# A four-layer transformer on one core: the fourth layer's bias in two one-pass parts, and maxima of two layers taken off over all 128 partitions

## The chip, the cores and the metric

The kernel runs on one core of a Trainium2 chip. The metric is the device time of one execution in microseconds (us), the median over several runs. A core has one engine for matrix products (TensorE, PE in the profile, with its weight loads as PEld), three for elementwise work (VectorE or DVE, ScalarE or ACT, GpSimd or POOL) and SyncE (SP), which here only issues DMA transfers.

## What is computed

Input `x` is (8, 512, 128) in float32: 8 batches of 512 tokens. Four layers follow, each `x = x + attention(norm(x)) + experts(norm(x))`. Layers 0, 2 and 3 have a softmax attention with 16 heads of 8 channels, layer 1 a linear attention. Layers 0 and 2 are causal; in layer 2 the masked scores are not left out of the softmax but set to a large negative number. Layer 3 is not causal and adds a relative bias:

```python
energy = jnp.einsum('bhqd,bhkd->bhqk', q, k)
rel = jnp.clip(pos[:, None] - pos[None, :] + (N - 1), 0, bias_table.shape[0] - 1)
energy = energy + bias_table[rel].transpose(2, 0, 1)[None]
att = jax.nn.softmax(energy / (scaling * temp), axis=-1)
out = jnp.einsum('bhqk,bhkd->bhqd', att, v)
```

The table has 249 rows, and the bias equals its last row unless the key lies more than 263 tokens ahead of the query. The kernel takes this constant off, so that a bias is left only in the last two of the four blocks of 128 keys, for the first 128 and the first 256 queries.

## The kernel before

**Units.** `attention` makes one layer's attention, and `run` (from line 501) orders it. A unit is one batch and one group of four heads, 32 units in a layer. A unit goes through half-steps x: six in a causal layer, eight in layer 3. A half-step handles one block of 128 keys or queries, or two short ones, for two of the four heads, so its tile in PSUM is a pair: two banks of 128 x 512 (`ps_pair`, three buffers, shared by everything that uses pairs).

**Two passes over the scores.** Five units ahead of the output (`AHEAD = 5`), `first` (line 273) computes the scores `s` with queries on the partitions, and `first_rest` (line 289) adds the causal mask and takes row maxima on VectorE into `max`. In layer 3 it also adds the bias table `far[0]` there, on VectorE, in the last half-steps. `maxima` and `turn_maxima` split the 16 heads' maxima of a batch into a high and a low part and transpose them to `mT`: on partition 32h + 2g is the high part of head h in group g, on the next the low part.

`second` (line 341) computes the scores again, transposed, with keys on the partitions, into `t`. The maxima are taken off by a product that accumulates into the same bank: a matrix `pick` of zeros and two rows of ones selects the high and low row of a head and spreads it over all 128 keys. `second_rest` (line 367) adds, in layer 3, the transposed bias by a product with the identity (line 376), in layer 0 a mask (line 382), and then ScalarE takes the exponential to `p` (line 386). In layer 2 the mask is a select on GpSimd after the exponential. `weigh` (line 397) multiplies `p` with the values, `finish` and `divide` evict, transpose and normalise.

**Precision and passes.** Queries and keys are stored as high and low parts in a rounded float type (F32R), four parts of 8 channels, 32 rows for each head. So `first`, `second` and the `pick` product contract over 32 of the array's 128 rows, in one pass, and the two heads of a half-step use different rows and can run at the same time; `first` takes the other two heads' rows. `far`, `ident`, `p` and the values are plain float32. The trace shows each float32 product as two instructions, each of them two passes over its columns.

**Order.** In the loop over units, a half-step issues `first` of the unit five ahead, `second` of the present one, then `first_rest` and `second_rest`, other tasks that are due (`now`), and `weigh` after some half-steps. The order on TensorE is the order of the calls. Other engines' order is left to a scheduler.

**Layer 3's table.** `load_far` loads each of two tables of 128 x 16 x 256 (2 MB) from SyncE, `scale_far` takes off the last row and scales, head by head on VectorE, in place. `far[0]` is used by `first_rest`, `far[1]` by `second_rest`. `choose` picks two experts for a batch in layer 3 and gathers their weights `ws`; `inner3` and `outer3` use them.

Of the kernel before, what the change touches and what calls it, by code (L numbers as in the profile page):

```python
# [22 lines left out]
P = 128  # L23
# [18 lines left out]
def network(ctx: ExitStack, tc: tile.TileContext, io: dict):  # L42
# [11 lines left out]
    def ps_pair(name):  # L54
        return ps.tile([P, 2, T], F32, tag="pair", name=name, bufs=3)
# [53 lines left out]
    nmx = const.tile([P, NI, P], F32, name="nmx")  # L109
    nc.gpsimd.memset(nmx, 0.0)  # L110

    pick = const.tile([P, NG, P], F32R, name="pick")
    pick32 = wk.tile([P, NG, P], F32, tag="oT", name="pick32")
    nc.gpsimd.memset(pick32, 0.0)
    for j in range(HG):
        for r in range(2):
            nc.gpsimd.affine_select(
                pick32, pick32, pattern=[[-2, NG], [0, P]], compare_op=ALU.not_equal, fill=1.0,
                base=-32 * j - r, channel_multiplier=1,
            )  # L120
# [49 lines left out]
    anchor = {}  # L170


    def attention(L, w, causal, scale, bias=None, soft=None, vpad=None, add_masks=False):

# [98 lines left out]
        def first(b, g, x):  # L273

            pr = 1 - x % 2
            q, k = st[b]["q", g], st[b]["k", g]
            s = st["s"] = ps_pair(f"s{L}_{b}_{g}_{x}")
            for j in range(2):
                r = 32 * (2 * pr + j)
                for i, c, n in spans(x, True)[0]:  # L280
                    nc.tensor.matmul(  # L281
                        s[:, j, c : c + n],
                        lhsT=q[r : r + 32, blk(i)],
                        rhs=k[r : r + 32, :n],
                        start=(c == 0),
                        stop=not causal,
                    )

        def first_rest(b, g, x):
            pr = 1 - x % 2  # L290
            m, s = st[b]["m"], st.pop("s")
            for i, c, n in spans(x, True)[0]:
                for j in range(2):
                    if causal:
                        nc.tensor.matmul(  # L295
                            s[:, j, c + n - P : c + n], lhsT=ident_bf, rhs=mask_qk, start=False,
                            stop=(i == spans(x, True)[0][-1][0]),
                        )
            for i, c, n in spans(x, True)[0]:
                e = 256 - 128 * i if bias is not None and i < 2 else 0  # L300
                anchor["vector"] = nc.vector.tensor_reduce(  # L301
                    m[:, i, g, 2 * pr : 2 * pr + 2], s[:, :, c : c + n - e], AX.X, ALU.max, negate=True
                ).ins
                for j in range(2 if e else 0):
                    h = 2 * pr + j
                    to = m[:, i, g, h : h + 1]
                    sum_ = small.tile([P, 256], BF16, tag="sum", name=f"sum{L}_{b}_{g}_{x}_{j}", bufs=1)
                    nc.vector.tensor_tensor_reduce(
                        sum_[:, :e], s[:, j, T - e : T], bias[0][:, g * HG + h, :e], -1.0, to, ALU.add, ALU.min, to
                    )  # L310
# [30 lines left out]
        def second(b, g, x):  # L341

            pr = x % 2
            q, key, mT = st[b]["q", g], st[b]["k", g], st[b]["mT"]
            s = st["t"] = ps_pair(f"t{L}_{b}_{g}_{x}")
            for k in range(2):
                r = 32 * (2 * pr + k)
                for j, c, n in spans(x, False)[0]:
                    nc.tensor.matmul(  # L349
                        s[:, k, c : c + n],  # L350
                        lhsT=key[r : r + 32, blk(j)],
                        rhs=q[r : r + 32, T - n : T],
                        start=(c == 0),
                        stop=False,
                    )
            for k in range(2):
                r = 32 * (2 * pr + k)
                for j, c, n in spans(x, False)[0]:
                    nc.tensor.matmul(  # L359
                        s[:, k, c : c + n],  # L360
                        lhsT=pick[r : r + 32, g, :],
                        rhs=mT[r : r + 32, T - n : T],
                        start=False,
                        stop=(j == pieces[x][-1] and not add_masks and not (bias is not None and j >= 2)),
                    )

        def second_rest(b, g, x):
# [3 lines left out]
            if bias is not None and pieces[x][0] >= 2:  # L371
                (j,) = pieces[x]
                for k in range(2):
                    h = g * HG + 2 * pr + k
                    n = 128 * (j - 1)
                    nc.tensor.matmul(  # L376
                        s[:, k, :n], lhsT=ident, rhs=bias[1][:, h, 256 - n :], start=False, stop=True
                    )
            if add_masks:
                for j, c, n in blocks:  # L380
                    for k in range(2):
# [119 lines left out]
    def run(layers, tasks, soft, normed=None, begun=0):  # L501
# [22 lines left out]
        with tc.manual_schedule(engines={mybir.EngineType.PE}):  # L524
# [9 lines left out]
            for u in range(AHEAD):  # L534
                _, b, g = units[u]
                for x in range(A.nh):
                    A.first(b, g, x)
                    A.first_rest(b, g, x)
                    if u == 1 and x == 0:
                        A.values(0)  # L540
                    if u == 1 and x == 3:
# [8 lines left out]
            for u, (A, b, g) in enumerate(units):  # L550
# [5 lines left out]
                for x in range(A.nh):  # L556
# [2 lines left out]
                        upto = -(-(x + 1) * F.nh // A.nh)  # L559
                        firsts, done = range(done, upto), upto  # L560
                    for y in firsts[:-1]:
                        F.first(fb, fg, y)
                        F.first_rest(fb, fg, y)
                    if firsts:
                        F.first(fb, fg, firsts[-1])
                    A.second(b, g, x)
                    if firsts:
                        F.first_rest(fb, fg, firsts[-1])
# [630 lines left out]
    att_w[3] = load_attention(3)  # L1199

    sizes = [("base", D), ("d1", 256)]
    f2 = lay.tile([P, sum(n for _, n in sizes)], F32, tag="weights", name="f2")
    cut, at = {}, 0
    for k, n in sizes:
        cut[k] = f2[:, at : at + n]
# [92 lines left out]

    last = l3.tile([P, NH], F32, name="last")
    nc.sync.dma_start(last, bcast_rows(io["a3_last"], NH))  # L1300
    far = [l3.tile([P, NH, 256], F32, name=f"far{k}") for k in range(2)]

    def load_far(k):
        nc.sync.dma_start(far[k], io["a3_far"][k])
# [10 lines left out]
    layer3 = attention(3, att_w[3], False, 1.0, bias=far, vpad=layer2.vpad)  # L1315

    f3s = {}

    def choose(b):
# [38 lines left out]

    def more23(at):
        for k in range(2):  # L1360
            at(1, 3 * k, load_far, k)
            for h in range(NH):
                at(4, 2 * (NH * k + h), scale_far, k, h)
        for b in range(NB):
# [107 lines left out]
```

## Time and profile before

Three runs took 2850.75, 2855.13 and 2861.95 us, median 2855.13. The profiled execution took 2855.47 us with a span of 2853.8 us. By stretches of its span, from the trace:

| us | what runs | TensorE busy, us | VectorE busy, us | ScalarE busy, us | granted clock of TensorE |
|---|---|---|---|---|---|
| 0 to 91 | opening: first scores of layer 0, routing | 56 | 69 | 12 | 0.69 |
| 91 to 485 | layer 0, attention | 356 | 224 | 156 | 0.79 |
| 485 to 903 | layer 0, attention with its experts | 359 | 89 | 208 | 1.00 |
| 903 to 962 | layer 0, end of attention | 48 | 11 | 29 | 0.69 |
| 962 to 1600 | layer 1 | 565 | 399 | 167 | 0.93 |
| 1600 to 1675 | layer 1 to 2 | 58 | 53 | 9 | 0.71 |
| 1675 to 2264 | layer 2, and first scores of layer 3 | 515 | 363 | 311 | 0.87 |
| 2264 to 2773 | layer 3 | 468 | 373 | 288 | 0.98 |
| 2773 to 2854 | end of layer 3 | 73 | 7 | 48 | 0.98 |

The granted clock is a mean over a stretch; in the trace it is 1 or 0.5 at any moment, so a mean of 0.79 says that 42% of the stretch ran at half clock. A matmul's duration in the trace is its latency, and matmuls overlap; how long a group holds the engine is read from the distance between starts. Costly groups that the change touches, by line: L359 (maxima, `t<-mT,pick`) 1536 matmuls, 265.1 us busy; L376 (bias, `t<-far,ident`) 256 of 256 columns and 256 of 128, 72.4 and 47.4 us; L386 (exponential) 640, 596.5 us; L301 (row maxima) 768, 664.7 us.

### The profile page before, as it was taken

Reading aid. Unit: us, or ns where it says so; the run is one execution under the profiler, and the core shown is the slowest. Engines: PE = TensorE matmul, PEld = TensorE weight load, DVE = VectorE, ACT = ScalarE, POOL = GpSimd, SP = SyncE. Lnnn points to the kernel's source line nnn. Section 1 sums busy time; section 2 is a strip of 40 time slices with the busy share of each in tenths; the row PEclk is TensorE's granted clock in tenths of the full one; section 3 lists DMA queues with packets and bytes.
Section 4 is the critical chain, followed back from the end, with each engine's and each line's share of the span. In section 5 each row is a group of like instructions: output and inputs, shape, how many; then the busy total and the mean of one; then the engine's idle time right before and its main releaser. Section 6 shows DMA issues by size and latency. Waiting matters only on the chain.

```text
span 2853.8 us, 45040 instructions
## 1 busy us (share of the span) xinstructions
PE 2498.7 (88%) x17094; PEld 1581.6 (55%) x17094; DVE 1587.6 (56%) x4014; ACT 1227.0 (43%) x1791; POOL 557.5 (20%) x742
## 2 busy tenths in 40 slices
PE   5889998888887888879999788888988899999999
PEld 3555555777775466667887654444443344444444
DVE  7666444222212376755555675666656677777760
ACT  1333444454454423212222135555654455555555
POOL 3006740000002255250000223333322200000000
PEclk7587789999999788899999778999898899999999
DMA  8314432555553211122232422222111111221200
GB/s 283 115 60 136 127 96 85 161 169 164 163 167 104 68 46 50 27 78 64 89 92 72 153 80 64 66 65 65 62 61 61 51 38 62 67 65 62 67 23 8
DMA packets 168633, 252.38 MB, mean 88 GB/s; under 512 B 21472, under 2 KB 92384, under 8 KB 168032
## 3 DMA queue, kind: packets, MB, share of 16 engines
q1 hardware_dynamic: 155744, 221.39, 24.9%
q0 software_dynamic: 12672, 28.10, 3.5%
q8 instruction: 136, 2.23, 0.3%
q14 instruction: 81, 0.66, 0.1%
HBM read 155.57 MB, written 93.85 MB: 87 GB/s over the span
## 4 chain that ended last, share of the span: by engine, by line
PE 46%; DVE 12%; ACT 4%; issue 3%; POOL 2%; DMA 2%; SPq 0%; POOLq 0%; ACTq 0%; DVEq 0%
PE o L403 6%; DVE max L301 5%; PE o L1046 5%; PE s L281 4%; PE t L376 3%; PE s L1023 3%; PE t L349 3%; PE rc L1247 3%; PE t L359 3%; PE qk L994 2%; PE y L757 2%; PE p L221 1%; PE h L961 1%; PE s L295 1%; PE h L963 1%
## 5 line engine op out<-in xcount | busy, mean ns | idle before, releaser
L301 DVE TENSOR_REDUCE max<-s 128x2 f32<-128x1024 f32 (+3 forms) x768 | 664.7, 885 | 399.2 <-PE s L295 278.1
L386 ACT ACTIVATE p<-t 128x1024 f32<-128x1024 f32 (+1 forms) x640 | 596.5, 938 | 580.5 <-PE t L382 228.3
L349 PE MATMUL t<-q,k 32*128 32x512 f32 (+3 forms) x1536 | 325.5, 452 | 100.0 <-ACT p L386 51.3
L281 PE MATMUL s<-k,q 32*128 32x512 f32 (+3 forms) x1536 | 328.9, 457 | 31.7 <-DMA k<-apartk 13.8
L403 PE MATMUL o<-p,vpad 128*32 128x512 f32 (+3 forms) x3072 | 347.9, 540 | 5.5 <-DVE at L440 3.2
L281 PEld LDWEIGHTS s<-k,q 32*128 32x128 f32 x1536 | 147.1, 204 | 320.4 <-issue 166.8
L771 POOL DMA_INDIRECT yk<-ys_d,slots x160 | 162.5, 1016 | 700.7 <-DMA ys_d<-y 520.9
L359 PE MATMUL t<-mT,pick 32*128 32x512 f32 (+3 forms) x1536 | 265.1, 370 | 0.0
L349 PEld LDWEIGHTS t<-q,k 32*128 32x128 f32 x1536 | 148.0, 202 | 189.9 <-ACT p L386 81.2
L757 PE MATMUL y<-wt,h 128*128 128x128 f32 x1632 | 202.7, 278 | 23.1 <-DVE xsT L746 14.0
L757 PEld LDWEIGHTS y<-wt,h 128*128 128x128 f32 x1632 | 192.6, 192 | 33.7 <-issue 16.4
L723 POOL DMA_INDIRECT xs_d<-xr,slots x160 | 157.5, 985 | 189.6 <-DVE slots L715 136.5
L854 ACT ACTIVATE h<-h,wt 128x256 f32<-128x256 f32 x316 | 122.4, 477 | 135.7 <-issue 126.5
L1046 PEld LDWEIGHTS o<-v,a 128*128 128x128 f32 x1280 | 158.1, 197 | 27.4 <-issue 27.3
L852 PE MATMUL h<-xsT,wt 128*128 128x256 f32 x632 | 153.1, 385 | 21.7 <-DVE xsT L746 14.8
L390 POOL TENSOR_SCALAR_AFFINE_SELECT p<-p 128x256 f32<-128x256 f32 x256 | 101.8, 410 | 314.4 <-ACT p L386 313.1
L1046 PE MATMUL o<-v,a 128*128 128x65 f32 x1280 | 161.3, 279 | 0.0
L859 DVE TENSOR_TENSOR y<-y,wt 128x256 f32<-128x256 f32 x79 | 33.5, 424 | 218.9 <-PE y L757 215.6
L359 PEld LDWEIGHTS t<-mT,pick 32*128 32x128 f32 x1536 | 153.0, 210 | 1.2 <-issue 0.5
L1033 DVE TENSOR_TENSOR a<-s,decay 128x1024 f32<-128x1024 f32 (+3 forms) x128 | 99.9, 816 | 84.0 <-PE s L1023 83.6
L403 PEld LDWEIGHTS o<-p,vpad 128*32 128x32 f32 x3072 | 71.3, 113 | 134.5 <-issue 100.9
L295 PE MATMUL s<-mask_qk,ident_bf 128*128 128x128 bf16 x1024 | 140.9, 249 | 0.0
(258 smaller groups left out, 3591.5 us busy)
## 6 DMA issues: line engine op xcount, KB each, us to landing
wt<-in_f_w SPq DMA_DIRECT2D x79, 578.0 KB, 3.9
q<-apartq SPq DMA_DIRECT2D x96, 256.0 KB, 2.7
k<-apartk SPq DMA_DIRECT2D x96, 256.0 KB, 3.7
wt<-in_f_w SPq DMA_DIRECT2D x23, 768.0 KB, 5.0
xs<-xs_d SPq DMA_DIRECT2D x102, 128.0 KB, 3.2
ys_d<-y SPq DMA_DIRECT2D x102, 128.0 KB, 4.0
xs_d<-zero SPq DMA_DIRECT2D x50, 256.0 KB, 5.1
apartq<-highq SPq DMA_DIRECT2D x48, 256.0 KB, 2.9
```

The source lines that it names most:

```text
L281: nc.tensor.matmul(s[:, j, c : c + n], lhsT=q[r : r + 32, blk(i)], rhs=k[r : r + 32, :n], start=(c == 0), stop=not causal,)
L295: nc.tensor.matmul(s[:, j, c + n - P : c + n], lhsT=ident_bf, rhs=mask_qk, start=False, stop=(i == spans(x, True)[0][-1][0]),)
L301: anchor["vector"] = nc.vector.tensor_reduce(m[:, i, g, 2 * pr : 2 * pr + 2], s[:, :, c : c + n - e], AX.X, ALU.max, negate=True).ins
L349: nc.tensor.matmul(s[:, k, c : c + n], lhsT=key[r : r + 32, blk(j)], rhs=q[r : r + 32, T - n : T], start=(c == 0), stop=False,)
L359: nc.tensor.matmul(s[:, k, c : c + n], lhsT=pick[r : r + 32, g, :], rhs=mT[r : r + 32, T - n : T], start=False, stop=(j == pieces[x][-1] a ...
L386: nc.scalar.activation(p[:, :, :width], s[:, :, :width], AF.Exp, scale=scale)
L403: nc.tensor.matmul(st[b, g][blk(h, 32), T - n : T], lhsT=vpad[b % 2][:, j, g * HG + h, :], rhs=st[b, g, j, h // 2][:, h % 2, :], start=(j ...
L723: ins = nc.gpsimd.indirect_dma_start(out=xs_d, out_offset=bass.IndirectOffsetOnAxis(ap=slots[:, b * NI + i, k : k + 1], axis=0), in_=state ...
L757: nc.tensor.matmul(py[:, blk(k)], lhsT=h[:, f, blk(k)], rhs=out(wt)[:, f, :], start=(f == 0), stop=(f == 3))
L771: nc.gpsimd.indirect_dma_start(out=yk[:, k, :], out_offset=None, in_=ys_d, in_offset=bass.IndirectOffsetOnAxis(ap=slots[:, b * NI + i, k : ...
L852: nc.tensor.matmul(s[:, f, :], lhsT=wt[:, blk(f)], rhs=xsT, start=True, stop=True)
L1046: nc.tensor.matmul(o[:, k, i * 65 : i * 65 + 65], lhsT=lin[b, c, "a", j][:, k, blk(i - j)], rhs=v1[b % 2][:, j, 2 * c + k, :], start=(j == ...
```

## The change

- `pick` becomes a matrix of 128 partitions x 4 heads x 4 groups. A column of it is repeated 128 times by a broadcast read. In layers 0 and 2 (`whole=True`) the product that takes the maxima off contracts over all 128 partitions, with ones in the two rows of its head and zeros elsewhere; in layer 3 (`whole=False`) it stays on 32.
- The transposed bias of layer 3 is held as a high and a low part in F32R (`far_high`, and `far_low` with `far_rest`), and each is added by a one-pass product with an F32R identity. The second table comes in head by head, into a buffer of tag `oT`, which the evicted outputs use too, and is scaled and split on VectorE.
- In the opening of a run of layers, `first` is called for two half-steps before their `first_rest`.
- `f2` moves to another pool; the weights `ws` have two buffers in place of four, and `choose` runs at half-step 1 of unit u - 1 in place of half-step 3 of unit u - 2, counted from the batch's first unit.

```diff
-    pick = const.tile([P, NG, P], F32R, name="pick")
-    pick32 = wk.tile([P, NG, P], F32, tag="oT", name="pick32")
+    pick = const.tile([P, HG, NG], F32R, name="pick")
+    pick32 = const.tile([P, HG, NG], F32, name="pick32")
...
+            m = P if whole else 32
             for k in range(2):
-                r = 32 * (2 * pr + k)
+                r = 0 if whole else 32 * (2 * pr + k)
                 for j, c, n in spans(x, False)[0]:
                     nc.tensor.matmul(
                         s[:, k, c : c + n],
-                        lhsT=pick[r : r + 32, g, :],
-                        rhs=mT[r : r + 32, T - n : T],
+                        lhsT=pick[r : r + m, 2 * pr + k, g : g + 1].to_broadcast([m, P]),
+                        rhs=mT[r : r + m, T - n : T],
                         start=False,
...
                     n = 128 * (j - 1)
-                    nc.tensor.matmul(
-                        s[:, k, :n], lhsT=ident, rhs=bias[1][:, h, 256 - n :], start=False, stop=True
-                    )
+                    for part in range(2):
+                        nc.tensor.matmul(
+                            s[:, k, :n], lhsT=bias[2], rhs=bias[1](h)[part][:, 256 - n :], start=False, stop=part == 1
+                        )
...
                 for x in range(A.nh):
-                    A.first(b, g, x)
-                    A.first_rest(b, g, x)
+                    if x % 2 == 0:
+                        pairs = [A.first(b, g, x), A.first(b, g, x + 1)]
+                    A.first_rest(b, g, x, pairs[x % 2])
...
-    far = [l3.tile([P, NH, 256], F32, name=f"far{k}") for k in range(2)]
+    far = l3.tile([P, NH, 256], F32, name="far")
+    far_high = l3.tile([P, NH, 256], F32R, name="far_high")
+    rest = lay.tile([P, 10 * 256], F32R, tag="weights", name="far_rest")
+    low = (rest[:, : 9 * 256].rearrange("p (h c) -> p h c", h=9), l3.tile([P, 7, 256], F32R, name="far_low"))
+    ident_r = rest[:, 9 * 256 : 9 * 256 + P]
+    nc.gpsimd.tensor_copy(ident_r, ident)
...
     def scale_far(k, h):
-        t = far[k][:, h, :]
+        if k == 0:
+            nc.vector.tensor_scalar(far[:, h, :], far[:, h, :], last[:, h : h + 1], rsc, ALU.subtract, ALU.mult)
+            return
+        t = wk.tile([P, 256], F32, tag="oT", name=f"far_{h}")
+        nc.sync.dma_start(t, io["a3_far"][1][:, h, :])
         nc.vector.tensor_scalar(t, t, last[:, h : h + 1], rsc, ALU.subtract, ALU.mult)
+        nc.vector.tensor_copy(far_high[:, h, :], t)
+        nc.vector.tensor_tensor(low[h // 9][:, h % 9, :], t, far_high[:, h, :].bitcast(F32), ALU.subtract)
...
-        ws = f3s[b] = [weights_of(io["f3_ch"], place, l3, "ws", 4, f"{n}_{k}") for k, place in enumerate((first, second))]
+        ws = f3s[b] = [weights_of(io["f3_ch"], place, l3, "ws", 2, f"{n}_{k}") for k, place in enumerate((first, second))]
...
-            at(u - 2, 3, choose, b)
+            at(u - 1, 1, choose, b)
```

More of the change, by code (lines that the diff above doesn't have):

```diff
@@ L110, in network @@
     nc.gpsimd.memset(nmx, 0.0)
-    pick = const.tile([P, NG, P], F32R, name="pick")
-    pick32 = wk.tile([P, NG, P], F32, tag="oT", name="pick32")
+    pick = const.tile([P, HG, NG], F32R, name="pick")
+    pick32 = const.tile([P, HG, NG], F32, name="pick32")
     nc.gpsimd.memset(pick32, 0.0)
[L115 to L119, printed above, removed]
-            )
+    for r in range(2):
+        nc.gpsimd.affine_select(
+            pick32, pick32, pattern=[[-32, HG], [-2, NG]], compare_op=ALU.not_equal, fill=1.0, base=-r,
+            channel_multiplier=1,
+        )
     nc.gpsimd.tensor_copy(pick, pick32)
@@ L170, in network, with attention @@
     anchor = {}
-    def attention(L, w, causal, scale, bias=None, soft=None, vpad=None, add_masks=False):
+    def attention(L, w, causal, scale, bias=None, soft=None, vpad=None, add_masks=False, whole=True):
         st = {}
@@ L276, in first @@
             q, k = st[b]["q", g], st[b]["k", g]
-            s = st["s"] = ps_pair(f"s{L}_{b}_{g}_{x}")
+            s = ps_pair(f"s{L}_{b}_{g}_{x}")
             for j in range(2):
@@ L287, in first, with first_rest @@
                     )
-        def first_rest(b, g, x):
+            return s
+        def first_rest(b, g, x, s):
             pr = 1 - x % 2
-            m, s = st[b]["m"], st.pop("s")
+            m = st[b]["m"]
             for i, c, n in spans(x, True)[0]:
@@ L375, in second_rest @@
                     n = 128 * (j - 1)
-                    nc.tensor.matmul(
-                        s[:, k, :n], lhsT=ident, rhs=bias[1][:, h, 256 - n :], start=False, stop=True
-                    )
+                    for part in range(2):
+                        nc.tensor.matmul(
+                            s[:, k, :n], lhsT=bias[2], rhs=bias[1](h)[part][:, 256 - n :], start=False, stop=part == 1
+                        )
             if add_masks:
@@ L561, in run @@
                     for y in firsts[:-1]:
-                        F.first(fb, fg, y)
-                        F.first_rest(fb, fg, y)
+                        F.first_rest(fb, fg, y, F.first(fb, fg, y))
                     if firsts:
-                        F.first(fb, fg, firsts[-1])
+                        s = F.first(fb, fg, firsts[-1])
                     A.second(b, g, x)
                     if firsts:
-                        F.first_rest(fb, fg, firsts[-1])
+                        F.first_rest(fb, fg, firsts[-1], s)
                     A.second_rest(b, g, x)
@@ L1201, in network @@
     sizes = [("base", D), ("d1", 256)]
-    f2 = lay.tile([P, sum(n for _, n in sizes)], F32, tag="weights", name="f2")
+    f2 = l3.tile([P, sum(n for _, n in sizes)], F32, name="f2")
     cut, at = {}, 0
@@ L1300, in network, with far_parts @@
     nc.sync.dma_start(last, bcast_rows(io["a3_last"], NH))
-    far = [l3.tile([P, NH, 256], F32, name=f"far{k}") for k in range(2)]
+    far = l3.tile([P, NH, 256], F32, name="far")
[4 more added lines that the diff above has]
+    nc.gpsimd.tensor_copy(ident_r, ident)
+    def far_parts(h):
+        return far_high[:, h, :], low[h // 9][:, h % 9, :]
     def load_far(k):
-        nc.sync.dma_start(far[k], io["a3_far"][k])
+        nc.sync.dma_start(far, io["a3_far"][0])
     def scale_far(k, h):
-        t = far[k][:, h, :]
+        if k == 0:
[3 more added lines that the diff above has]
+        nc.sync.dma_start(t, io["a3_far"][1][:, h, :])
         nc.vector.tensor_scalar(t, t, last[:, h : h + 1], rsc, ALU.subtract, ALU.mult)
+        nc.vector.tensor_copy(far_high[:, h, :], t)
+        nc.vector.tensor_tensor(low[h // 9][:, h % 9, :], t, far_high[:, h, :].bitcast(F32), ALU.subtract)
     wr3 = const.tile([D, 8], F32, name="wr3")
@@ L1313, in network @@
     nc.sync.dma_start(br3, bcast_rows(io["f3_br"], 8))
-    layer3 = attention(3, att_w[3], False, 1.0, bias=far, vpad=layer2.vpad)
+    layer3 = attention(3, att_w[3], False, 1.0, bias=(far, far_parts, ident_r), vpad=layer2.vpad, whole=False)
     f3s = {}
@@ L1360, in more23 @@
         for k in range(2):
-            at(1, 3 * k, load_far, k)
+            if k == 0:
+                at(1, 0, load_far, k)
             for h in range(NH):
```

## The prediction

> **What bounds the kernel now.** I read the page first: TensorE's share, then the row of its granted clock.
>
> ```profile
> PE 2498.7 (88%) x17094; PEld 1581.6 (55%) x17094; DVE 1587.6 (56%) x4014; ACT 1227.0 (43%) x1791; POOL 557.5 (20%) x742
> ...
> PEclk7587789999999788899999778999898899999999
> ```
>
> TensorE is the bound at 88%, but its clock is not full in the slices of layer 0 (1 to 6), around 13 and in layer 2 (23 to 31). So I asked for the busy time by stretches: three attention units of layer 0 with the same work (g = 2 of three batches).
>
> ```profile
> 269.92:287.96 18.04, 16.40 (x119) 9.24 (x118) 8.52 (x19) 5.77 (x7) 13.65 (x15) 0.62 0.29 98
> 335.07:350.21 15.14, 13.78 (x118) 7.91 (x118) 8.31 (x19) 5.83 (x8) 11.48 (x13) 0.77 0.27 90
> 456.36:469.30 12.94, 11.29 (x118) 6.51 (x118) 8.13 (x19) 5.76 (x7) 0.00 (x0) 1.00 0.14 45
> ```
>
> The columns are length, busy time and count of PE, PEld, DVE, ACT and POOL, granted clock, DMA share and GB/s. Equal counts of matmuls take 12.94, 15.14 and 18.04 us at clocks 1.00, 0.77 and 0.62. The clock is either 1 or 0.5, so 0.62 means that 76% of 18.04 us (13.7 us) ran at half clock: each us at half clock loses (18.04 - 12.94)/13.7 = 0.37 us (the middle unit: 2.2/7.0 = 0.31). I take 0.36.
>
> What sets it? The clock changes on a grid of 3.41 us; three cells of it:
>
> ```profile
> 280.56:283.97 3.41, 3.41 (x25) 2.08 (x21) 1.38 (x4) 0.60 (x1) 2.80 (x3) 0.50 0.21 65
> 283.97:287.38 3.41, 3.41 (x28) 1.44 (x26) 1.06 (x3) 0.60 (x1) 2.49 (x4) 0.50 0.66 211
> 287.38:290.79 3.41, 2.66 (x26) 1.26 (x26) 1.97 (x2) 1.60 (x2) 2.50 (x4) 1.00 0.12 38
> ```
>
> In the first, TensorE has no gap at all and stays at half clock; only after the second is it full. Busy time is not what counts. The first cell holds, by form: 8 score products of 256 columns and 4 maxima products of 256, all on 32 of 128 rows, 5 masks and 4 two-pass transposes of 128 columns on all rows, and part of a group of 32-column products. I weighted each matmul by its share of the array, columns x passes x rows/128 x output columns/128, over the 8192 columns that a cell passes at full clock (a 512-column pass takes 0.215 us, from 1.72 us for the four two-pass products of L1340). The first cell gives 0.34, the second 0.405. Over all of the trace's cells this one number sorts the clock of the next cell: below 0.37 it is half, above it full, right in 99% of the cells at full and 97% of those at half clock. That is my reading of this trace, and most of the forecast rests on it.
>
> The other part lies in layer 3 (2264 to 2854 us), nearly always at full clock (0.98), with PE busy 468 of 509 us. First a half-step there, then one of layer 2:
>
> ```profile
> 2507.59 0.40 PE L359 MATMUL t<-mT,pick 32*128 32x512 f32 x2
> 2507.92 1.13 PE L376 MATMUL t<-far,ident 128*128 128x256 f32 x4
> 2508.98 0.50 PE L281 MATMUL s<-k,q 32*128 32x512 f32 x2
> ...
> 1900.76 0.50 PE L349 MATMUL t<-q,k 32*128 32x512 f32 x2
> ...
> 1901.10 0.39 PE L359 MATMUL t<-mT,pick 32*128 32x512 f32 x2
> ...
> 1901.42 0.11 PEld L295 LDWEIGHTS <-ident_bf 128*128 128x128 bf16 x2 [0.36 <-issue]
> ```
>
> Read the distance of the starts: the bias product of two heads takes 1.06 us at 256 columns (0.55 at 128); the maxima of two heads take 0.32 at 512, of which 0.215 is one pass (both heads at once, on different rows) and about 0.11 is the change of rows.
>
> [...]
>
> **The maxima in layers 0 and 2.** Per half-step the pair on 32 rows becomes two products on 128 rows, one after the other[...]. At 512 columns: 2 x 0.215 = 0.43 for 0.32, +0.11. At 384 + 128: 0.43 for 0.38 (1905.50 to 1905.88), +0.05. At 256: 0.215 for 0.21, nothing. Two half-steps of each in a unit: +0.32 us. PE waits for ACT 25 us of layer 0's attention and 22 of layer 2, so I put 60% on the path: 0.2 x 64 units = +13.
> The array share of these products becomes four times as large: in layer 0 they are 0.03 of a cell's 0.43, so 0.09 is added. The first cell above goes from 0.34 to 0.43: full clock. I laid the trace's matmuls out again with this share, the lengths above and the rule at 0.37. Layer 0's attention (91 to 485 us) goes from 165 us at half clock (2 x 0.21 x 394) to some 15, and its end (903 to 962) from 37 to 16; layer 2 (1675 to 2264, clock 0.87) from 153 to some 65. That is 259 us less, x 0.36 = -93. I keep 80% of it, since ACT and DVE, hidden behind a slow TensorE, come due: -74. Together with +13: -61.
>
> **The bias in layer 3.** A 256-column bias of two heads now is four products of one pass: 0.055 for the first weights, 4 x 0.11, 0.09 to drain: 0.58 for 1.06, -0.48. At 128: 0.35 for 0.55, -0.2. Two of each in a unit: -1.36 us, x 32 units = -43. DVE is late next: its half-steps here take 1.74 us (0.69 + 2 x 0.48 + 0.08), and PE's go from about 2.2 and 1.7 to 1.7 and 1.5. It waits for DVE already:
>
> ```profile
> PE t L349 <- DVE max L301: 17.9, 23, 1.4
> ...
> PE t L349 <- DVE max L308: 6.0, 14, 0.8
> ```
>
> The third buffer of pairs and the four light half-steps of a unit catch part; I count 75%: -32. The bias loses half of its array share, 0.07 of a cell's 0.59; laid out again, layer 3 has 10 to 20 us more at half clock: +5. No row shows a 128-row one-pass product in this type: bounds are one pass (taken, since 128 columns of it on 32 rows take as long as bf16's, 0.055) and two passes (no gain here).
>
> **The rest.** Splitting the table: 16 heads at 0.40 (the present scaling) plus a copy and a subtraction of that size, about +13 us of DVE in units 9 to 14, where it has room. Each scaling waits for a DMA of 128 KB issued beside it, landing in about 3 us, in a buffer shared with the evicted outputs: behind it on DVE queue the maxima, behind the buffer ACT's eviction, and on SP the q and k loads, a unit early. From 0 to 16 x 3 = 48; I take +6. The one 2 MB load becoming 16, the choice of experts three quarters of a unit later (two weight buffers; its landing of 2.8 us still has more than a unit), eight mask builds less on POOL (0.63 each, ahead of a gather at 19 us that waits for a DMA), the moved tile of 384 columns and the copy of the identity: nothing, -5 to +5. Pairs of first products in the opening: 15 times two products at once, DVE busy 29 of 35 us there: 0 to -5, I take 0.
>
> **Sum.** -61 - 32 + 5 + 6 = -82. The profiled execution took 2855.47 us, practically the median, 2855.13: 2773.
>
> **Rivals.** (A) As summed, 2773, its own range 2735 to 2815; 70%. (B) The clock hardly follows, because what is counted is not rows but something that goes with them in this trace: +13 - 43 x 0.75 + 6 = -13, 2842; with half of the clock's gain 2805; 12%. For it: the rule is a fit. Against: without the row share it sorts 92% of the cells at full and two thirds of those at half clock. (C) Layer 3 falls below the threshold: once at half clock, a cell with less than 0.37 keeps it there; at 200 us, +72 - 5 on top, 2840; 7%. Against: the median cell is at 0.59. (D) Slower: full-height one-pass products take two passes. The pair at 512 would be 0.86, 2.5 us more in a unit, x 64 x 0.6 = +95, with all of layer 3's gain gone, and the clock's -74: +27, 2882. It decides above 1.7 passes. 7%. (E) The table's DMAs hold up DVE at their upper bound: 2815; 4%.
>
> **How the numbers follow.** 0.5% (14 us) is what a measurement of this kernel tells from no change. Faster by more: A, C's better half, E, most of B: 0.86. Within: 0.07. Slower: D, 0.07. The range takes A with B's half gain and E: 2730 to 2825.
>
> **What would show it.** Clock of 91 to 485 above 0.93 (right) or still near 0.79 (B); starts of the two maxima products 0.215 apart (0.43: D); 512-column pair plus mask 0.11 later than before; the 256-column bias near 0.58; more waits of L349's line for DVE; layer 3's clock at 0.96 or more (below 0.9: C). I am wrong if the clock rises and units do not shorten.

## The result, and the profile after

The changed kernel took 2889.86 us in the median of nine runs (2867.96 to 2916.23), the kernel before 2854.87 us in as many (2840.2 to 2861.95): a ratio of 1.0119, 95% interval 1.0088 to 1.015. It is slower by 35 us, where 82 us less were forecast. A ratio here and below is an estimate over fast runs (three slow ones among the experiments are left out) and need not be the quotient of the two medians. The profiled execution took 2889.86 us too, with a span of 2888.2.

The page of the changed kernel, TensorE's share and the row of its clock in 40 slices:

```profile
PE 2534.7 (88%) x17094; PEld 1630.7 (56%) x17094; DVE 1607.2 (56%) x4046; ACT 1225.6 (42%) x1791; POOL 553.1 (19%) x737
...
PEclk7789999999999888899999789999999998999999
```

Slices 2 to 7 (layer 0) and those of layer 2 hold more nines than before: the clock rose where it was meant to. Yet TensorE is busy 36 us longer with the same number of instructions. The view by stretches (length, busy time and count of each engine, clock, DMA share, GB/s) for layer 0's attention, layer 2 and layer 3 of the changed kernel:

```profile
84.80:484.20 399.40, 360.60 (x3010) 223.35 (x3008) 223.47 (x553) 155.15 (x202) 133.00 (x136) 0.91 0.31 96
...
1684.70:2286.90 602.20, 540.01 (x3719) 292.42 (x3718) 384.71 (x909) 310.39 (x481) 182.03 (x329) 0.95 0.20 64
2286.90:2878.50 591.60, 538.81 (x3460) 250.21 (x3462) 384.56 (x974) 334.12 (x363) 21.42 (x20) 0.93 0.16 51
```

Cut at the first exponential of each layer, which both traces have, the stages compare so (us, clock in brackets; the forecast column is the prediction's own terms, sorted by stage, clock gain at 80%):

| stage | before | after | difference | forecast |
|---|---|---|---|---|
| opening | 91.3 | 84.8 | -6.5 | 0 |
| layer 0, attention alone | 393.7 (0.79) | 399.4 (0.91) | +5.7 | |
| layer 0, attention with experts, and end | 476.1 | 483.7 | +7.6 | |
| layer 0 together | 869.8 | 883.1 | +13.3 | -43 |
| layer 1 | 713.7 | 716.7 | +3.0 | 0 |
| layer 2 | 589.3 (0.87) | 602.2 (0.95) | +12.9 | -13 |
| layer 3 | 579.9 (0.98) | 591.6 (0.93) | +11.7 | -27 |

Two things need a cause: layers 0 and 2 run at a higher clock and still take longer, and layer 3, whose bias products became cheaper, takes longer at a lower clock.

**The maxima.** One half-step at full clock in the timeline of TensorE (start, time, engine, line, operation; the scores are recorded with 0.50 us, and the maxima start 0.34 after them), first the kernel before:

```profile
382.52 0.50 PE L349 MATMUL t<-q,k 32*128 32x512 f32 x2 [0.30 <-ACT p L386]
382.86 0.39 PE L359 MATMUL t<-mT,pick 32*128 32x512 f32 x2
383.18 0.28 PE L295 MATMUL s<-mask_qk,ident_bf 128*128 128x128 bf16 x2
```

and the same half-step of the changed kernel:

```profile
378.44 0.50 PE L351 MATMUL t<-q,k 32*128 32x512 f32 x2 [0.30 <-ACT p L390]
378.87 0.73 PE L362 MATMUL t<-mT,pick 128*128 128x512 f32 x2
379.44 0.29 PE L297 MATMUL s<-mask_qk,ident_bf 128*128 128x128 bf16 x2
```

From scores to mask it is 0.66 us before (382.52 to 383.18) and 1.00 after (378.44 to 379.44): +0.34, where the forecast had +0.11. The weight loads of the same two stretches say where it comes from, before:

```profile
382.63 0.19 PEld L359 LDWEIGHTS t<-mT,pick 32*128 32x128 f32 x2
```

and after:

```profile
378.87 0.30 PEld L362 LDWEIGHTS t<-mT,pick 128*128 128x128 f32 x2 [0.25 <-issue]
```

On 32 rows the weights of `pick` were loaded at 382.63, 0.11 us after the scores' start, while the scores were still running on the same rows (a head's scores and its maxima use the same 32), and both products start within 4 ns. On all rows the loads start only at 378.87, 0.43 us after the scores' start, together with the first product. They start 0.107 us apart, the two products 0.33 (378.87 and 379.20), and a pass of 512 columns is 0.215. So the half-step pays a second pass, 0.215, and a weight load, 0.107. The change of rows did not go away: from the last maxima product to the mask it is 0.23 us now, for 0.32, but from scores to maxima 0.43, for 0.34. The loads of the mask, in bf16, start about 0.056 apart. Why a full-height load starts so late behind products on 32 rows, no run shows.

Half-steps of 384 + 128 columns went from 0.72 to 1.05 (+0.33), those of 256 columns cost 0.21 more. Two of each in a unit make 1.76 us, not 0.32. Whole units at full clock confirm it: those of g = 1 in layer 0 went from 12.9 to 14.6 us and in layer 2 from 15.6 to 17.6, those of g = 2 in layer 2 from 14.5 to 15.9. Where the clock was already full before, the cost stands bare: the seventh batch of layer 0, which runs beside the experts, went from 418.3 to 422.8 us. In the four batches ahead of it, at 0.76 to 0.91 before, cost and clock came out even (245.3 us together before, 245.6 after).

### The profile page after: what moved, and what is told of

Its sections match the earlier page's. It is cut to its first block, busy times and chain, and to the rows that moved or that the text cites. A ratio compares the mean times of both kernels' runs of the same rounds, so it can differ in the third digit from the quotient of the medians.

```text
span 2888.2 us, 45104 instructions
## 1 busy us (share of the span) xinstructions
PE 2534.7 (88%) x17094; PEld 1630.7 (56%) x17094; DVE 1607.2 (56%) x4046; ACT 1225.6 (42%) x1791; POOL 553.1 (19%) x737
## 4 chain that ended last, share of the span: by engine, by line
PE 46%; DVE 11%; ACT 4%; issue 3%; DMA 3%; POOL 2%; SPq 0%; POOLq 0%; ACTq 0%; DVEq 0%
PE o L407 6%; DVE max L303 5%; PE o L1050 5%; PE t L362 4%; PE s L282 4%; PE s L1027 3%; PE t L351 3%; PE rc L1251 2%; PE t L380 2%; PE qk L998 2%; PE y L761 2%; ACT p L390 1%; PE h L965 1%; PE h L967 1%; PE v L991 1%
## 5 line engine op out<-in xcount | busy, mean ns | idle before, releaser
L303 DVE TENSOR_REDUCE max<-s 128x2 f32<-128x1024 f32 (+3 forms) x768 | 666.2, 887 | 418.3 <-PE s L297 303.0
L390 ACT ACTIVATE p<-t 128x1024 f32<-128x1024 f32 (+1 forms) x640 | 595.8, 937 | 645.3 <-PE t L386 247.0
L351 PE MATMUL t<-q,k 32*128 32x512 f32 (+3 forms) x1536 | 316.1, 439 | 100.7 <-ACT p L390 54.1
L362 PE MATMUL t<-mT,pick 32*128 32x512 f32 (+4 forms) x1536 | 378.2, 384 | 0.0
L282 PE MATMUL s<-k,q 32*128 32x512 f32 (+3 forms) x1536 | 313.7, 446 | 41.0 <-DVE max L303 19.5
L407 PE MATMUL o<-p,vpad 128*32 128x512 f32 (+3 forms) x3072 | 341.6, 531 | 4.8 <-DVE at L444 2.4
L282 PEld LDWEIGHTS s<-k,q 32*128 32x128 f32 x1536 | 139.5, 196 | 315.7 <-issue 137.9
L362 PEld LDWEIGHTS t<-mT,pick 128*128 128x128 f32 (+1 forms) x1536 | 212.8, 199 | 70.1 <-issue 39.1
L351 PEld LDWEIGHTS t<-q,k 32*128 32x128 f32 x1536 | 140.3, 191 | 195.1 <-ACT p L390 85.7
L761 PEld LDWEIGHTS y<-wt,h 128*128 128x128 f32 x1632 | 192.4, 192 | 32.9 <-issue 16.4
L856 PEld LDWEIGHTS h<-xsT,wt 128*128 128x128 f32 x632 | 113.8, 190 | 40.4 <-DVE xsT L750 25.3
```

The costliest lines, as they stand in the source:

```text
L282: nc.tensor.matmul(s[:, j, c : c + n], lhsT=q[r : r + 32, blk(i)], rhs=k[r : r + 32, :n], start=(c == 0), stop=not causal,)
L303: anchor["vector"] = nc.vector.tensor_reduce(m[:, i, g, 2 * pr : 2 * pr + 2], s[:, :, c : c + n - e], AX.X, ALU.max, negate=True).ins
L351: nc.tensor.matmul(s[:, k, c : c + n], lhsT=key[r : r + 32, blk(j)], rhs=q[r : r + 32, T - n : T], start=(c == 0), stop=False,)
L362: nc.tensor.matmul(s[:, k, c : c + n], lhsT=pick[r : r + m, 2 * pr + k, g : g + 1].to_broadcast([m, P]), rhs=mT[r : r + m, T - n : T], sta ...
L390: nc.scalar.activation(p[:, :, :width], s[:, :, :width], AF.Exp, scale=scale)
L407: nc.tensor.matmul(st[b, g][blk(h, 32), T - n : T], lhsT=vpad[b % 2][:, j, g * HG + h, :], rhs=st[b, g, j, h // 2][:, h % 2, :], start=(j ...
```

## The experiments

The expectations number four theories. 1: the maxima by themselves cost more than the higher clock returns. 2, its rival: they don't, and the loss lies elsewhere. 3: in layer 3, VectorE waits for the gathered weights of the chosen experts, TensorE waits behind it, and the clock falls. 4: the place of the choice of experts does it.

Seven of the twelve kernels ran on two other chips, where every kernel takes 7% longer (before: 3066 and 3060 us), mostly in pauses of layer 0's attention that I did not trace to a cause. Ratios compare runs of one chip only. Times of a layer have to be compared across chips, since the kernel before has a trace on one chip alone: layer 3 carries over to within a few us, layer 2 less well (the changed kernel took 602.2 us there, the same code with the late sum below 608.9 on another chip).

| kernel | before there, us | this, us | ratio, 95% interval |
|---|---|---|---|
| maxima only | 3066 | 3094.05 | 1.0088, 1.0063 to 1.0113 |
| all but the maxima | 3066 | 3083.17 | 1.0056, 1.0035 to 1.0076 |
| all, late sum | 3066 | 3115.81 | 1.0141, 1.01 to 1.0183 |
| all but the maxima, late sum | 3066 | 3076.01 | 1.0031, 1.001 to 1.0053 |
| wide masks only | 2849.17 | 2848.09 | 0.998, 0.9957 to 1.0003 |
| old place, two buffers, late sum | 2849.17 | 2901.26 | 1.0168, 1.0132 to 1.0204 |
| choice moved only | 2849.17 | 2869.17 | 1.0066, 1.0048 to 1.0084 |
| all but the maxima, old place | 3059.83 | 3070.27 | 1.0027, 1.001 to 1.0044 |
| all, old place | 3059.83 | 3094.18 | 1.01, 1.0072 to 1.0128 |
| all but the maxima, old place, wide masks | 3059.83 | 3062.19 | 1.0003, 0.9981 to 1.0025 |
| pairs and wide masks | 2854.46 | 2847.85 | 0.9967, 0.9948 to 0.9985 |
| pairs only | 2854.46 | 2848.85 | 0.9981, 0.9962 to 1.0 |

### Maxima alone, and everything but the maxima

The first is the kernel before with the new `pick` and the full-height product in layers 0 and 2:

```diff
-                r = 32 * (2 * pr + k)
+                r = 0 if whole else 32 * (2 * pr + k)
...
-                        lhsT=pick[r : r + 32, g, :],
-                        rhs=mT[r : r + 32, T - n : T],
+                        lhsT=pick[r : r + m, 2 * pr + k, g : g + 1].to_broadcast([m, P]),
+                        rhs=mT[r : r + m, T - n : T],
```

The second is the changed kernel with the product on 32 rows in all layers:

```diff
-    def attention(L, w, causal, scale, bias=None, soft=None, vpad=None, add_masks=False, whole=True):
+    def attention(L, w, causal, scale, bias=None, soft=None, vpad=None, add_masks=False, whole=False):
```

> The kernel before with one part of the change: the maxima of layers 0 and 2 taken off by products over all 128 rows; bias, table, opening and choice of experts as before. Theory 1 (the full-height products cost about 1.76 us in each of 64 units, because two run one after the other and the first one's weights are no longer loaded under the products before it; the higher clock gives back less): layers 0 and 2 each about 13 us longer, 2880 (2866 to 2895), clock of layer 0's attention near 0.92. Theory 2 (the loss comes from layer 3, its late gather and lower clock; the maxima pay for themselves): 2850 or less.

> The changed kernel with the maxima of layers 0 and 2 back on 32 rows, all else as changed. Theory 1: layers 0 and 2 are back at their times and clocks of before, layer 3 still some 12 us longer than before and the opening 6 us shorter: 2861 (2848 to 2872), clock of layer 3 still near 0.92. Theory 2: 2885 or more.

The maxima alone cost 0.9%, as expected, with layer 3 at 583.6 us and a clock of 0.97: theory 1 holds and theory 2 falls, for this part of the loss. Without them the change still loses 0.56%, more than the 0.2% expected, with layer 3 at 595.8 us. So layer 3 lost on its own. Reading the broadcast `pick` is not the reason: on 32 rows its products stand as far apart as before (0.34 and 0.32).

### The wait for the gathered weights

Both kernels move the sum of the two chosen experts' biases, which waits on VectorE for the gathered weights, to the place of its use in the program; the second is without full-height maxima too.

```diff
-        b2 = f3s["b2", b] = small.tile([P, 1], F32, tag="b2", name=f"b2{n}")
-        nc.vector.tensor_tensor(b2, ws[0][:, 2 * D + 1 :], ws[1][:, 2 * D + 1 :], ALU.add)
...
-        del f3s[b]
+        ws = f3s.pop(b)
+        b2 = f3s["b2", b] = small.tile([P, 1], F32, tag="b2", name=f"b23_{b}")
+        nc.vector.tensor_tensor(b2, ws[0][:, 2 * D + 1 :], ws[1][:, 2 * D + 1 :], ALU.add)
```

> The changed kernel with the sum of the two chosen experts' second biases moved from the choice to the last product of the experts, so that VectorE doesn't wait for the gathered weights in the middle of the fourth unit of a batch. Theory 3 (in layer 3 this wait is what empties TensorE for 2.5 us and drops the clock; the smaller array share only keeps it there for some cells): clock of layer 3 back to 0.97 or more, its batches 72 us in place of 77, 2860 (2848 to 2872). Rival (the smaller share of the bias products alone lowers the clock): clock stays at 0.92 to 0.94, 2885.

> Both of these edits: one-pass bias in two parts, maxima on 32 rows everywhere, late sum. Theories 1 and 3 together: opening -6, layer 3 -22 against before: 2828 (2812 to 2845), the fastest of all. If either is wrong: 2850 or more.

Layer 3 took 592.9 and 593.2 us at a clock of 0.93, as with the early sum, and both missed what theory 3 expected (2860 and 2828 us, for 2855). But these two kernels do not test theory 3: VectorE's order is the scheduler's, and it left the sum where it was. Here it is in the fourth unit of layer 3's first batch, 10 us into the unit, with the next product of TensorE that hangs on it, in the changed kernel:

```profile
2358.18 0.16 DVE L1353 TENSOR_TENSOR b<-ws,ws 128x1 f32<-128x1 f32 x1 [1.13 <-DMA ws<-in_f_ch,row]
...
2358.98 1.09 PE L153 MATMUL xd<-ident,dT 128*128 128x128 f32 x4 [2.42 <-DVE at L444]
```

and with the late sum:

```profile
2559.02 0.16 DVE L1368 TENSOR_TENSOR b<-ws,ws 128x1 f32<-128x1 f32 x1 [1.18 <-DMA ws<-in_f_ch,row]
...
2559.82 1.09 PE L153 MATMUL xd<-ident,dT 128*128 128x128 f32 x4 [2.48 <-DVE at L444]
```

VectorE waits for the gathered weights, the division that writes `at` stands behind the sum, and TensorE waits for `at`. That wait of TensorE over layer 3 (us in total, times, longest), before, in the changed kernel and with the late sum:

```profile
PE xd L153 <- DVE at L440: 8.2, 8, 1.1
```

```profile
PE xd L153 <- DVE at L444: 16.5, 8, 2.5
```

```profile
PE xd L153 <- DVE at L444: 18.0, 8, 2.6
```

In six of the seven fourth units in which the changed kernel has a choice, TensorE waits 2.3 to 2.5 us here, and in each of the six the clock falls to half between 10 and 13 us into the unit, at a grid point during this wait or soon after it. In the seventh the wait is 1.2 us; the clock had fallen earlier. So theory 3 was not tested by its own experiment, and the traces speak for it: TensorE waits 8 us longer here, and the falls of the clock follow this wait.

### The choice of experts moved alone, and moved back

The kernel before with one line of the change:

```diff
-            at(u - 2, 3, choose, b)
+            at(u - 1, 1, choose, b)
```

> The kernel before with one edit: the choice of experts moved to half-step 1 of a batch's fourth unit; bias and maxima as before. Theory 4: fourth units of layer 3 show half clock that they don't have before, but leave it again in the far half-steps, whose bias still counts fully: layer 3's clock 0.95 to 0.97, +5 us. Rival (the place doesn't matter): clock 0.98, ratio 1.000.

This line alone costs 0.66%, some 19 us where 5 were expected, and in the profiled run (2880.64 us, above its median) layer 3 goes from 579.9 to 598.9 us. The units where the choice now stands, the fourth of a batch, went from 18.5 us to between 20.2 and 22.5 in the first six batches, 20.2 where the clock stayed full; those it left, the third, from 17.6 to 17.1. Cells of the clock's grid in the kernel before, at the light half-steps of such a unit (no bias products in them):

```profile
2475.33:2478.74 3.41, 2.55 (x24) 0.95 (x20) 2.28 (x3) 2.44 (x3) 0.00 (x0) 1.00 0.18 62
2478.74:2482.16 3.42, 2.57 (x20) 0.88 (x16) 2.31 (x2) 2.51 (x4) 0.00 (x0) 1.00 0.00 0
```

and with the choice moved:

```profile
2484.39:2487.80 3.41, 2.56 (x26) 1.21 (x22) 3.02 (x7) 1.98 (x3) 0.00 (x0) 1.00 0.35 135
2487.80:2491.21 3.41, 3.31 (x16) 0.85 (x12) 2.08 (x9) 1.75 (x3) 1.02 (x1) 0.50 0.00 0
```

TensorE is busy 2.55 us in the first cell of each, and yet the next one is at full clock in one kernel and at half in the other. By the array share of the forecast, the first cell has 0.43 before and 0.34 with the choice. The choice puts a product of 8 columns between the maxima and the values, which takes TensorE 0.32 us and fills next to nothing, so the values' products, which use all rows, begin only as the cell ends; its chain of short VectorE operations (0.16 to 0.20 us each) then stands among the row maxima that TensorE needs. The clock is 0.77 over the 22 us of this unit, so some 10 us of it ran at half clock. Six of the seven units with a choice in layer 3 ran partly at half clock, and none of them before. Four of the six fell like this one, 2 to 3 us into the unit and ahead of the sum, whose wait for the weights is then gone. The other two fell right after TensorE's longer wait for `at` (2.4 and 1.9 us); the seventh had that wait too, 2.5 us, and kept its full clock. So the new place does harm in two ways, by the choice's own instructions and by the wait for its weights. In the changed kernel the second prevails, and no run separates them.

Three runs move the choice back to half-step 3 of unit u - 2. The first keeps two weight buffers and the late sum.

```diff
-            at(u - 1, 1, choose, b)
+            at(u - 2, 3, choose, b)
```

The others have room for four gathered weights as well: two lie in a buffer of layer 2 that is free by then. The sum is early, as in the kernel before; one is without full-height maxima, the other with them.

```diff
+        two = [None, None]
+        if b % 2:
+            both = l3.tile([P, 2, io["f3_ch"].shape[1]], F32, tag="dT", name=f"ws2_{n}")
+            two = [both[:, k, :] for k in range(2)]
```

> Like the one-pass bias with maxima on 32 rows and the late sum, but the choice of experts back in the third unit of a batch (half-step 3), as before the change. Theory 4 (the choice's twelve small VectorE steps in the light half-steps of the fourth unit, whose cells are at 0.41 and 0.42 before, push them below 0.37; the halved share of the bias then holds them there): layer 3's clock back to 0.96 or more, its batches 72 us, layer 3 some 15 us shorter than before, ratio 0.993 to 0.998. Rival (the halved share alone): clock stays near 0.92, ratio 1.003.

> The bias in two parts alone: maxima on 32 rows everywhere, and the choice of experts back at half-step 3 of unit u - 2 with room for four gathered weights (two in the old buffers, two in layer 2's adapter buffer, free by then). Theory 4 (layer 3's loss is the move of the choice, and the bias products themselves gain): layer 3 goes from about 580 to 560-570 us with a clock of 0.96 or more, layer 2 about 10 us longer for the table's pieces, the opening 6 shorter: a ratio of 0.992 to 0.998. Rival (the bias products' halved array share is what drops layer 3's cells to half clock, wherever the choice stands): layer 3 at 590 or more with a clock near 0.93, a ratio of 1.003 to 1.008.

> The whole change, with the choice of experts back at half-step 3 of unit u - 2 and room for four gathered weights. If costs add: the change's ratio of 1.012 less the 0.0066 that the move alone cost, 1.005 (2863 against 2850), with layer 3 at 565-575 us and layers 0 and 2 as in the changed kernel. Rival (halved array share): no more than 0.002 below the change, 1.010.

The first missed, because it made a wait of its own: the gather of one batch now needs the buffers of the batch before. The waits of VectorE and TensorE in its layer 3 (us in total, times, longest):

```profile
DVE b L1368 <- DMA ws<-in_f_ch,row: 19.8, 7, 4.2
```

```profile
PE t L351 <- DVE max L303: 32.9, 23, 4.7
```

VectorE stands 19.8 us for the weights, and behind it TensorE waits 32.9 us for row maxima. It says nothing of the place.

With four buffers, layer 3 takes 579.0 and 578.6 us, 13 to 14 less than with the new place (591.6 in the changed kernel, 593.2 and 592.9 in the two with the late sum), its fourth units take 17.7 us, the shortest of all kernels, and TensorE's wait for `at` is back at 8.4 us. The choice moved alone had four buffers throughout, so it is the place and not the room that counts: it is worth 13 us of layer 3. But the ratios are those of the rival (1.003 to 1.008 and 1.010), not of theory 4 (0.992 to 0.998 and 1.005), and the clock is 0.94, not 0.96: the halved share costs as well. Whole batches at full clock take 71.9 us there, 2.2 less than the 74.1 of before; others have units at half clock, such as this pair of cells of the run without full-height maxima:

```profile
2602.62:2606.03 3.41, 2.33 (x21) 0.94 (x20) 2.28 (x2) 3.40 (x4) 0.00 (x0) 1.00 0.26 94
2606.03:2609.45 3.42, 2.96 (x16) 1.34 (x12) 2.59 (x5) 2.11 (x3) 0.00 (x0) 0.50 0.00 0
```

Here the unit, 23.1 us, went to half clock in its light half-steps and stayed there; the same unit of the next batch did not, and took 17.3. Why the one fell and the other did not, no run shows.

What the cheaper bias brings at full clock is seen in the timeline of a half-step, before:

```profile
2433.84 1.13 PE L376 MATMUL t<-far,ident 128*128 128x256 f32 x4
2434.90 0.50 PE L281 MATMUL s<-k,q 32*128 32x512 f32 x2
2435.61 0.50 PE L349 MATMUL t<-q,k 32*128 32x512 f32 x2 [0.21 <-DVE max L308]
```

and with the bias in two parts and the choice at its old place:

```profile
2732.82 0.39 PE L380 MATMUL t<-far_high,far_rest 128*128 128x256 f32 x1
2733.04 0.28 PE L380 MATMUL t<-far_rest 128*128 128x256 f32 x1
2733.16 0.28 PE L380 MATMUL t<-far_high,far_rest 128*128 128x256 f32 x1
2733.28 0.28 PE L380 MATMUL t<-far_rest 128*128 128x256 f32 x1
2733.49 0.50 PE L282 MATMUL s<-k,q 32*128 32x512 f32 x2
2734.59 0.50 PE L351 MATMUL t<-q,k 32*128 32x512 f32 x2 [0.60 <-DVE max L310]
```

The bias takes 0.67 us for 1.06. But the next `t` starts 1.77 us after the first bias product in both: all 0.39 go into a longer wait for VectorE's row maxima. The following half-step keeps its 0.39. At 128 columns the two heads' bias went from 0.55 to 0.50 only, since the products start 0.11 us apart, for 0.12 at 256: each has a weight load of its own, and in the changed kernel's trace these start 0.109 us apart at 128 columns and 0.117 at 256.

### A higher clock by another way

The kernel before with the causal mask of the first scores added over 256 columns (128 of them zeros) where the scores have that many. The products are in one pass on all rows, so the array share rises at an estimated 0.056 us each, the distance at which the mask products of 128 columns start in the kernel before. With it comes the small `pick`, on 32 rows. The second kernel adds the same to the run with the bias in two parts and the choice at its old place.

```diff
-                            s[:, j, c + n - P : c + n], lhsT=ident_bf, rhs=mask_qk, start=False,
+                            s[:, j, c + n - m2 : c + n], lhsT=ident_bf, rhs=mask_wide[:, 2 * P - m2 :], start=False,
```

> The kernel before (with the maxima's selection matrix read by broadcast, still on 32 rows), and in layers 0 and 2 the mask products on the first scores 256 columns wide in place of 128 where the block has as many, with zeros in the added half: nothing else changes, each half-step passes 256 more columns over the whole array and takes 0.11 us more. If the clock follows the share of the array used (0.37 of a 3.41 us cell): half-clock time of layer 0's attention falls from 42% to about 22% and its clock rises to 0.88 or so, layer 2's to 0.91, and the time comes out even, ratio 0.995 to 1.006. [...]

> The bias in two parts with the choice at its old place, and the causal masks of the first scores widened to 256 columns with zeros, which raises the array share of layers 0 and 2 without full-height maxima. The wide masks alone were even (0.998), so about 0.002 below the run without them: 0.990 to 0.996. It is the candidate to beat both kernels. If layer 3 stays at half clock in a quarter of its cells, 1.001 to 1.006.

Layer 0's attention and layer 2 of the first kernel:

```profile
92.90:492.40 399.50, 360.39 (x3008) 217.39 (x3006) 224.32 (x553) 155.24 (x201) 132.88 (x136) 0.83 0.31 96
...
1689.50:2275.90 586.40, 518.21 (x3720) 266.68 (x3719) 364.03 (x865) 310.95 (x481) 180.77 (x329) 0.90 0.20 62
```

Zeros on the array raised the clock from 0.79 to 0.83 and from 0.87 to 0.90, less in layer 0 than expected (0.88), and the time is even, as expected. TensorE's busy share of the two stretches stayed as it was (0.90 for 0.90, 0.88 for 0.87), so it is not what raised the clock. The threshold of 0.37 sorts this trace too (99% of the cells at full clock and 99% of those at half). A product that only fills the array paid here for about what it brought. The second kernel came out 0.24% below the run without wide masks (1.0003 for 1.0027, overlapping intervals). It missed the 0.990 to 0.996 expected of it: layer 3, at a clock of 0.94, took 583.4 us.

### Pairs of first products in the opening

The one part of the change that shows a gain in the whole time, though alone only at the edge of its interval:

```diff
-                    A.first(b, g, x)
-                    A.first_rest(b, g, x)
+                    if x % 2 == 0:
+                        pairs = [A.first(b, g, x), A.first(b, g, x + 1)]
+                    A.first_rest(b, g, x, pairs[x % 2])
```

> The kernel before with two parts alone: first products called in pairs in the opening, and the causal masks of the first scores 256 columns wide with zeros on the left. Maxima, bias and choice of experts as before. If the opening's 6 us come from the pairs and the wide masks stay even (0.998 alone): a ratio of 0.995 to 0.997, below 1 with its whole interval, with layer 3 at 580 us. Rival (the opening's gain belongs to the rows of the maxima or is taken back by layer 0's first units): 0.998 to 1.000, opening at 91 us.

> The kernel before with first products called in pairs in the opening, nothing else. If the pairs are what shortened the opening: opening at 85 us for 91, and a ratio of 0.997 to 0.999. Rival (they are not): opening at 91 us and a ratio of 1.000.

The opening before, and then with pairs only:

```profile
0.00:91.30 91.30, 56.69 (x245) 33.52 (x246) 68.71 (x220) 12.27 (x22) 23.55 (x50) 0.69 0.81 269
```

```profile
0.00:86.60 86.60, 46.74 (x246) 30.36 (x247) 67.99 (x220) 12.19 (x22) 23.53 (x50) 0.70 0.85 284
```

VectorE has the same 68 us of work in 4.7 us less; as I read it, two products at once let it start sooner. Alone the ratio is 0.9981, with an upper end at 1.0. With wide masks it is 0.9967, below 1 with its whole interval: this kernel is faster than the one before by 0.3%, the expected size. It can't be told from either of its parts alone, whose intervals overlap with its own.

## Why the prediction was wrong

The forecast named its own sign of being wrong, and it came: the clock rose and the units did not shorten.

**The clock (right in its mechanism, seven tenths of its size).** Forecast: 259 us less at half clock, kept at 80%, -74. Measured from the clock's records: layer 0's attention 165 to 68 us (forecast 15), its end 35 to 31 (16), layer 2 149 to 66 (65): 184 us less, x 0.36 = -66 if all of it is kept. The array share sorts the cells of the changed trace too (98% of those at full clock, 91% of those at half), so it is the place that fell short, layer 0. I had kept the lengths of before when laying out the new shares; longer units thin out the share in each cell. That is argued, not run.

**The maxima (the step that failed).** "At 512 columns: 2 x 0.215 = 0.43 for 0.32, +0.11 ... +0.32 us" in a unit, 60% of it on the path, +13. That counts two passes and nothing else: the 0.1 us of the change of rows was taken to end with the products on 32 rows, and no weight load was added. It measured 1.76 us in a unit. The change of rows did not go but moved ahead of the product (0.43 for 0.34), and the second product starts 0.33 us after the first, a pass and a weight load of 0.107. Of 113 us in 64 units, an estimated 50 in layer 0 and about 35 in layer 2 stand on the path (the stage differences with the clock's gain, and in layer 2 the table's part below, taken out): +85 for +13. The number of passes was bounded from both sides, the load and the change of rows were not. Their nearest case, a full-height product behind one on 32 rows, was in the trace: in each group of 256-column bias products the first is 0.32 us ahead of the next, the others 0.216.

**The bias (mechanism right, size off).** Forecast 0.58 for 1.06 and 0.35 for 0.55, 1.36 us in a unit, 75% of it kept, -32. Measured 0.67 and 0.50 to 0.59, some 0.87 in a unit, of which 0.55 came through, -18. The first weights took 0.105 us for the 0.055 forecast (in the changed kernel's trace the second product starts 0.223 after the first, the next 0.118 later), and a 128-column product 0.112 for 0.055, with weight loads that start 0.109 apart; the 0.09 at the end was right (0.21 from the last product to the next scores, 0.12 of it the product's). VectorE was late next, as said.

**The halved array share in layer 3 (mechanism right, size off).** Forecast +5. With the choice at its old place the clock is 0.94; with the old bias it is 0.97 in the run of the maxima alone and 0.98 in the kernel before: 34 to 44 us more at half clock, +12 to +16 by the same 0.36.

**The choice of experts (counted as nothing).** "The choice of experts three quarters of a unit later ... nothing, -5 to +5", because the landing of 2.8 us "still has more than a unit". It had not: the sum of the two biases uses the weights at once, VectorE waited up to 1.2 us for them in the middle of a unit and 4.1 in the last, and TensorE behind it 8 us more than before. What counted besides was where the choice's instructions went: into half-steps of 0.42, near the threshold of 0.37. It cost 13 us in the change and 19 alone. So layer 3's account is -18 + 16 + 13 = +11, for 11.7 measured.

**The table.** Forecast +6; it was not run alone. Layer 2 without full-height maxima took 600.6 us on another chip for 589.3, +11, nearly all in its third and fourth batch, where the scaling stands. On one chip, that of the choice moved alone (592.4), the run with two buffers took 598.1, +6. So it is between 6 and 11.

**The opening.** Forecast 0 of a range of -5 to 0; measured -6.5.

**The rivals.** (D) had nearly the time, 2882, but for another reason: full-height products take one pass (two of 512 columns start 0.33 us apart, a weight load of 0.107 included, where two passes take 0.43). (C), layer 3 falling below the threshold, came true in part: 34 to 44 us more at half clock by the halved share, some 20 by the choice. The parts of the change do not simply add: maxima, choice and the rest measured alone, 0.0088 + 0.0066 + 0.0027, make 0.018 for a change of 0.012. Back at its old place in the full change, the choice returned 0.004 (1.0141 to 1.01, overlapping intervals; the first with the late sum and on another chip) and not 0.0066; this was not resolved.

## What to carry to other kernels

Where a product goes from a few rows to all of them, count every start distance from the product ahead to the one behind: the second pass (0.215 us here), the weight load (0.107), and the row change (0.1), which here did not go but moved. When a granted clock below 1 is the loss, price what raises it against what a us at half clock returns (0.36 us here); filling the array at its own cost came out even (0.998), and where the clock is full already it is pure loss (418.3 to 422.8 us in a batch of layer 0). A task that moves is to be judged by the stage it moves into and by who stands behind its waits: the moved choice cost 13 us, most of the 18 that the cheaper bias brought. And look in the trace whether an edit moved what it was meant to move, before a theory is dropped for it.

## What the runs showed of the hardware

- How much of the array is used, not how busy TensorE is, went with the next cell's clock: cells of 2.55 busy us led to full clock at a share of 0.43 and to half clock at 0.34, and zeros added to the masks raised the clock from 0.79 to 0.83.
- Behind scores on 32 rows, the weights of a full-height F32R product start to load 0.43 us after the scores' start, and the second product starts 0.33 us after the first: a pass, 0.215, and a weight load, 0.107. On the same 32 rows as the scores, the weights start to load 0.11 us after them, and the two products of a pair start within 0.03 us.
- One-pass F32R products with a weight load each start 0.112 us apart at 128 columns and 0.12 at 256, so the first cost nearly as much as the second; the mask's bf16 products of 128 columns, with a load each, start 0.056 apart.
